# Attention weights turned for two heads at once: 64 places of the context per head, and the 13 left of eight heads together

## The chip, the core and the metric

The kernel runs on one core of a Trainium2 chip, in one launch, all in float32. The metric is the device time of the program in microseconds (us), as the median of several runs. Beside it there is one execution taken by the hardware profiler, with its own time and a trace of every instruction. The engines are called by the names of the profile: PE is TensorE's matmul and PEld its weight load, DVE is VectorE, ACT is ScalarE, POOL is GpSimd, SP the engine that only starts DMAs.

## The reference

Sixteen sequences of 128 rows of 128 numbers attend, with 16 heads of 8 numbers, to a context of 77 places of 96 numbers each. The result goes, behind a gate, into a mixture of four experts in four rounds, which the change does not touch. What it computes before that, cut to the attention:

```python
q = (einsum('bld,ed->ble', layernorm(x), Wq) + bq).reshape(b, l, 16, 8)
kv = (einsum('bmc,ec->bme', ctx, Wkv) + bkv).reshape(b, 77, 16, 16)
k, v = kv[..., :8], kv[..., 8:]
att = softmax(einsum('blhd,bmhd->blmh', q, k) / sqrt(8), axis=2)      # over the 77 places
out = einsum('blmh,bmhd->blhd', att, v).reshape(b, l, 128)
x = x + tanh(g_xattn) * (einsum('bld,ed->ble', out, Wo) + bo)
# then layernorm, and four rounds of: gate to 2 of 4 experts, gelu MLP 128 -> 512 -> 128, add
```

## The kernel before

The order of the work on PE, DVE and ACT is written out by hand: each engine runs its instructions in the order in which the program issues them, and so does GpSimd where the helper `gp` (line 88) records them. What one engine waits for from another is a semaphore.

The attention stage is a loop over the 16 sequences (line 1039), one round each, with the work of several sequences in flight. In round b:

- `spread_keys(b + 2)` on GpSimd makes `km`, the keys of a sequence once for each of four heads of a group, with the other heads' numbers zeroed (line 753).
- `turn_weights` (line 804) turns the weights of sequence b. `ex` holds, for 128 rows, 16 heads of 77 exponentials. PE transposes each head, 128x77 to 77x128, four heads to a bank of PSUM, and ACT copies each bank (77x512) to `exT`. The first two groups go before the scores of sequence b + 1, the other two after them. There are two banks for it (`bank_tr`), which `put_out` uses too.
- `scores(b + 1)` (line 766): four products of 32 rows, each in a group of rows of PE, two banks for each half.
- `put_out(b - 1)`: the output product of the sequence before; DVE adds it to x.
- `weights(b + 1)` (line 785), in two halves of eight heads: DVE takes the maximum of each head (L791), subtracts it into `ex` (L795), ACT takes the exponential in place (L801).
- `attend(b)` (line 811): 32 products of 77 places. Each puts 32 of the 128 rows of the result, so four of them stand side by side on PE. Half of them multiply by ones (`one`) and give the sums of the weights, half by the values (`vm`, in which the eight numbers of a head stand among zeros). Four heads of a group add up in one place of PSUM.
- `over_sums(b)` (line 829): DVE's reciprocal of the sums (L831) and the product with it (L833).

Work for later sequences is hung into the rounds with the lists `early` (between the first turned groups and the scores), `extra` (after the last turned group), `amid` and `behind` (after `attend` and after `over_sums`). There, each four sequences (i = 0 to 3) get their context turned (`turn_ctx`, line 710: four transposes, one copy by ACT into `ctxT`), their keys (`keys`, one product and one copy), queries and values (`values`, line 740: four products with the turned context as weights, four copies by ACT into `vm[i % 2]`). DVE and GpSimd also do, from round 7 on, the gate of the experts' first round. Products of these helpers take turns in two banks of PSUM (`bank`, line 114), so each new one waits until the one before the last has been read.

Before the loop the same helpers are called for the first four sequences (lines 846 to 876), with `warm` products that do nothing between them, and `spread_rows` (line 878) makes row constants: DVE copies them out (L885), ACT takes a tanh (`tg`, L886), DVE makes `bo_b` (L887), ACT copies `woT` and `wgT`.

Of the kernel before, what the change touches and what calls it, by code (L numbers as in the profile page):

```python
# [24 lines left out]
F32 = mybir.dt.float32  # L25
I32 = mybir.dt.int32
AF = mybir.ActivationFunctionType
ALU = mybir.AluOpType
# [3 lines left out]
P = 128  # L32
NH = 16
DH = 8
# [12 lines left out]
def gated_xattn_moe(  # L47
# [20 lines left out]
    nc = tc.nc  # L68
    B, L, D = x.shape
    M, C = ctx_768.shape[1:]  # L70
# [3 lines left out]
    BB = 4  # L74
    NB = B // BB
    TB = BB * L
# [18 lines left out]
    gp = Pinned()  # L95
# [29 lines left out]
    wkT = const.tile([C + 1, D], F32, name="wkT")  # L125
    wvT = const.tile([C + 1, D], F32, name="wvT")
# [8 lines left out]
    ident = const.tile([P, P], F32, name="ident")  # L135
# [34 lines left out]
    HG = 4  # L170
    NG = NH // HG
    GW = HG * DH
# [19 lines left out]
    akeep = ctx.enter_context(tc.tile_pool(name="akeep", bufs=1))  # L192


    vm = [akeep.tile([M, BB, HG * (D + DH)], F32, name=f"vm{i}") for i in range(2)]
    for i in range(2):
        nc.vector.memset(vm[i], 0.0)

    nc.vector.tensor_reduce(
        hmask,  # L200
        ident.rearrange("p (g k d) -> p k g d", k=HG, d=DH),
        AX.XY,
        ALU.add,
    )
    ctxT = akeep.tile([C + 1, B, M], F32, name="ctxT")
    gp.memset(ctxT[C : C + 1, :, :], 1.0)
    one = akeep.tile([M, HG, GW], F32, name="one")
    gp.memset(one, 0.0)
    for k in range(HG):
        gp.memset(one[:, k, ts(k, DH)], 1.0)  # L210
    gp.memset(blk, 0.0)


# [45 lines left out]
    awork = ctx.enter_context(tc.tile_pool(name="awork", bufs=2))  # L259

    def mm(*args, **kw):
        nc.tensor.matmul(*args, **kw)  # L262

    def tp(*args):
        nc.tensor.transpose(*args)  # L265
# [415 lines left out]
    ps = bank("ps_wkv")  # L681
# [28 lines left out]
    def turn_ctx(i):  # L710
        ps = bank("ps_ct")
        for j in range(BB):
            tp(ps[:C, ts(j, M)], ctx_sb[:, i * BB + j, :], ident[:M, :M])
        nc.scalar.copy(
            ctxT[0:C, ts(i, BB), :].rearrange("c b m -> c (b m)"), ps[:C, : BB * M]
        )

    def keys(i):
        ps = bank("ps_k")
        mm(  # L720
            ps[:, : BB * M], wkT, ctxT[:, ts(i, BB), :].rearrange("c b m -> c (b m)"),
            start=True, stop=True,
        )
        nc.scalar.copy(kT[:, ts(i, BB), :].rearrange("d b m -> d (b m)"), ps[:, : BB * M])

# [9 lines left out]
    def queries(i):  # L735
        ps = bank("ps_q")
        mm(ps, wqT, xnTs.pop(i), start=True, stop=True)
        nc.scalar.activation(qT[i], ps, AF.Identity, bias=bqc)

    def values(i):  # L740
        ps = bank("ps_v")
        for j in range(BB):
            mm(ps[:M, ts(j, D)], ctxT[:, i * BB + j, :], wvT, start=True, stop=True)
        for j in range(BB):

            nc.scalar.copy(
                vm[i % 2][:, j, :]
                .rearrange("m (k n) -> m k n", k=HG)[:, :, 0:D]
                .rearrange("m k (g n) -> m k g n", g=NG)[:, :, :, 0:DH],
                ps[:M, ts(j, D)].rearrange("m (g k d) -> m k g d", g=NG, k=HG),  # L750
            )
# [14 lines left out]
    def scores(b, km):  # L766


        q = qT[b // BB][:, ts(b % BB, L)]
        scs = []  # L770
        for u in range(2):
            sc = banks2("sc")
            for g in range(2):
                at = slice((2 * u + g) * GW, (2 * u + g + 1) * GW)
                mm(
                    sc[:, g, : HG * M],
                    q[at, :],
                    km[at, :, :].rearrange("d h m -> d (h m)"),
                    start=True,
                    stop=True,  # L780
                )
            scs.append(sc)
        return scs

    def weights(scs, then=None):

        ex = awork.tile([P, NH, M], F32, tag="ex", name="ex")
        for u, sc in enumerate(scs):
            sv = sc[:, :, : HG * M].rearrange("l g (h m) -> l g h m", m=M)
            mx = small.tile([P, 2, HG], F32, tag="mx", name="mx")  # L790
            beats.append(nc.vector.tensor_reduce(mx, sv, AX.X, ALU.max))  # L791
            if u and then:
                then()
            eu = ex[:, ts(u, 2 * HG), :]
            nc.vector.tensor_tensor(  # L795
                eu.rearrange("l (g h) m -> l g h m", h=HG),
                sv,
                mx.unsqueeze(3).to_broadcast([P, 2, HG, M]),
                ALU.subtract,
            )  # L800
            nc.scalar.activation(eu, eu, AF.Exp, scale=1.0 / math.sqrt(DH))  # L801
        return ex

    def turn_weights(ex, exT, groups):
        for g in groups:
            ps = bank_tr("ps_tr")
            for j in range(HG):
                tp(ps[:M, ts(j, L)], ex[:, g * HG + j, :], ident)
            nc.scalar.copy(exT[:, ts(g, HG), :].rearrange("m h l -> m (h l)"), ps[:M, :])  # L809

    def attend(b, exT):


        ps = bank("ps_av")
        for w in range(2):
            for k in range(HG):
                for g in range(NG):
                    at = slice(g * GW, (g + 1) * GW)
                    mm(
                        ps[at, ts(w, L)],  # L820
                        one[:, k, :] if w == 0
                        else vm[b // BB % 2][:, b % BB, k * D + g * GW : k * D + (g + 1) * GW],
                        exT[:, g * HG + k, :],
                        start=(k == 0),
                        stop=(k == HG - 1),
                    )
        return ps

    def over_sums(ps):
# [14 lines left out]


    turn_ctx(0)
    warm(2)
    keys(0)
    ps = bank("ps_cols")
# [21 lines left out]
    warm(4)  # L871
    scs = scores(0, kms.pop(0))
    values(0)
    turn_ctx(1)
    ex = {0: weights(scs)}
    keys(1)

# [41 lines left out]
    extra = {b: [] for b in range(B)}  # L919
# [119 lines left out]
    for b in range(B):  # L1039
        if b + 2 < B:  # L1040
            kms[b + 2] = spread_keys(b + 2)
        exT = awork.tile([M, NH, L], F32, tag="exT", name="exT")
# [12 lines left out]

        if b + 1 < B:
            ex[b + 1] = weights(scs, put_before)
        else:
            put_before()
        if b:  # L1060
            stats_x1(b - 1)
        ps_av = attend(b, exT)
        if b == B - 1:

            junk = const.tile([1, 1], F32, name="junk")
            nc.scalar.activation(junk, zero[0:1, 0:1], AF.Gelu_apprx_tanh)
            turn_half(0, 0, state[0]["c"])
        for f in amid[b]:
            f()
        o[b] = over_sums(ps_av)  # L1070
        for f in behind[b]:
            f()

        n = len(beats)
        for k in range(3):
            if (b, k) in stores_at:
                scatter(0, first["pos"], stores_at[b, k], stores, beats[n - 3 + k])
        if b == 14:
            load(0, stores)
# [280 lines left out]
```

## Time and profile before

| | |
|---|---|
| median of 3 runs | 449.91 us (449.91 to 450.17) |
| profiled execution, its own time | 448.24 us |
| its span, first to last instruction | 446.4 us |
| mean granted PE clock | 0.994 |
| attention stage, first turned weights to the last `over_sums` | about 19.3 to 115.8 us |

The page's first three parts:

```profile
PE 430.0 (96%) x4506; PEld 405.3 (91%) x4506; DVE 346.5 (78%) x918; ACT 274.8 (62%) x853; POOL 214.4 (48%) x249
PE   6899999998999999999999999999999999999991
DVE  8489998998866996897698689858867986774561
ACT  2567766766655666566666656666665666666661
POOL 5561926157005934752592377158426814650061
```

A digit is the busy share of a fortieth of the span, 11.16 us, in tenths. The attention stage is the first ten digits. A product in float32 is two records (two passes) in the trace, a transpose one. A record of PE lasts 0.27 us or more, but the next one starts much earlier, so the time of a row of products is read from their starts, as the chain of waits does.

The groups of instructions that the change touches, over the whole execution (columns: line, engine, operation, out<-in, shapes, count; busy us and mean ns of one; idle us before and what ended it):

```profile
L809 ACT COPY exT<-ps_tr 77x512 f32<-77x512 f32 x64 | 34.0, 581 | 13.4 <-PE ps_tr L265 13.1
L265 PE MATMUL ps_tr<-ident,ex 128*77 128x128 f32 x256 | 35.1, 280 | 1.1 <-ACT exT L809 1.1
L801 ACT ACTIVATE ex<-ex 128x616 f32<-128x616 f32 x32 | 23.0, 719 | 13.7 <-DVE ex L795 13.4
L791 DVE TENSOR_REDUCE mx<-sc 128x8 f32<-128x616 f32 x32 | 25.3, 790 | 5.8 <-PE sc L262 5.7
L795 DVE TENSOR_TENSOR ex<-sc,mx 128x616 f32<-128x616 f32 x32 | 25.4, 794 | 1.5
```

### The profile page before, as it was taken

To read this page: it belongs to the slowest core of one execution; us is meant where nothing else is said; L and a number is where in the kernel's file an instruction comes from. 1 tells how busy PE (TensorE), PEld (TensorE's weight loads), DVE (VectorE), ACT (ScalarE), POOL (GpSimd) and SP (SyncE) were. 2 spreads that over 40 slices of the span, in tenths; PEclk is the share of its full clock that TensorE was granted. 3 is DMA by queue.
4 is the path that set the end of the run, shared out by engine and by line. 5 is a ranking of instruction groups with operands and counts; after the bars stand their busy time and mean duration, and the time that the engine had idled before them with its cause. 6 is when DMAs were issued, how large, how long until landed. Compare 5 with 4: busy or idle time off the path is not lost.

```text
span 446.4 us, 12234 instructions
## 1 busy us (share of the span) xinstructions
PE 430.0 (96%) x4506; PEld 405.3 (91%) x4506; DVE 346.5 (78%) x918; ACT 274.8 (62%) x853; POOL 214.4 (48%) x249
## 2 busy tenths in 40 slices
PE   6899999998999999999999999999999999999991
PEld 6677888877899999999999999999999999999991
DVE  8489998998866996897698689858867986774561
ACT  2567766766655666566666656666665666666661
POOL 5561926157005934752592377158426814650061
PEclk9999999999999999999999999999999999999997
DMA  7520000012202301300130122014002201410000
GB/s 166 184 96 4 1 3 1 1 40 76 84 3 74 121 2 51 122 28 3 72 123 1 38 73 88 1 63 135 2 26 73 98 3 63 134 42 8 1 35 14
DMA packets 19553, 24.08 MB, mean 54 GB/s; under 512 B 3940, under 2 KB 16550, under 8 KB 19366
## 3 DMA queue, kind: packets, MB, share of 16 engines
q1 hardware_dynamic: 14868, 13.41, 9.6%
q0 software_dynamic: 3648, 9.71, 6.0%
q8 instruction: 36, 0.59, 0.5%
q10 hardware_dynamic: 978, 0.18, 0.2%
q14 instruction: 23, 0.19, 0.1%
HBM read 13.58 MB, written 9.71 MB: 52 GB/s over the span
## 4 chain that ended last, share of the span: by engine, by line
PE 71%; issue 9%; DVE 8%; POOL 6%; DMA 4%; ACT 1%; POOLq 0%; ACTq 0%; DVEq 0%
PE ps_y L262 28%; PE ps_h L262 28%; POOL out_dram L1124 4%; PE ps_av L262 4%; PE ps_tr L265 4%; DVE mx L791 2%; DMA wall<-in_L_ffn_W_dram 2%; DVE ex L795 2%; PE ps_c L265 2%; DVE rs L831 1%; PE sc L262 1%; DMA ctx_sb<-in_ctx_dram 1%; PE ps_bh L262 1%; DMA wq_n<-in_L_xattn_Wq_dram 1%; ACT exT L809 1%
## 5 line engine op out<-in xcount | busy, mean ns | idle before, releaser
L1096 ACT ACTIVATE hT<-ps_h,wb 128x128 f32<-128x128 f32 x512 | 145.9, 368 | 81.6 <-ACT hT L1096 56.7
L262 PE MATMUL ps_h<-curT,wb 128*128 128x128 f32 x1024 | 135.4, 275 | 0.7 <-ACT curT L379 0.7
L262 PE MATMUL ps_y<-wb,hT 128*128 128x128 f32 x1024 | 135.7, 276 | 0.0
L262 PEld LDWEIGHTS ps_h<-curT,wb 128*128 128x128 f32 x1024 | 124.6, 192 | 0.9 <-ACT curT L379 0.9
L262 PEld LDWEIGHTS ps_y<-wb,hT 128*128 128x128 f32 x1024 | 124.5, 192 | 0.0
L522 POOL DMA_INDIRECT sorted<-rows,pos_i x64 | 69.9, 1092 | 112.2 <-DVE start L515 49.3
L1015 DVE COPY wb<-wall 128x1028 f32 x128 | 105.4, 826 | 12.7 <-issue 6.5
L93 POOL TENSOR_TENSOR lp<-rows,wg_rows 128x512 f32<-128x512 f32 x48 | 75.3, 1593 | 29.7 <-DVE rows L1110 27.5
L1110 DVE SCALAR_TENSOR_TENSOR rows<-ps_y,pws,rows 128x128 f32<-128x128 f32 x126 | 43.6, 346 | 33.9 <-PE ps_y L262 33.9
L1096 ACT ACTIVATE hT<-ps_h,wall 128x128 f32<-128x128 f32 x160 | 45.7, 368 | 32.6 <-PE ps_h L262 32.6
L262 PE MATMUL ps_y<-wall,hT 128*128 128x128 f32 x320 | 43.1, 278 | 0.0
L262 PE MATMUL ps_h<-cx,wall 128*128 128x128 f32 x320 | 42.3, 275 | 0.0
L809 ACT COPY exT<-ps_tr 77x512 f32<-77x512 f32 x64 | 34.0, 581 | 13.4 <-PE ps_tr L265 13.1
L262 PEld LDWEIGHTS ps_y<-wall,hT 128*128 128x128 f32 x320 | 38.9, 192 | 2.7 <-ACT hT L1096 2.7
L262 PEld LDWEIGHTS ps_h<-cx,wall 128*128 128x128 f32 x320 | 38.9, 192 | 0.0
L265 PEld LDWEIGHTS ps_tr<-ident,ex 128*77 128x77 f32 x256 | 27.9, 147 | 10.1 <-ACT exT L809 7.8
L265 PE MATMUL ps_tr<-ident,ex 128*77 128x128 f32 x256 | 35.1, 280 | 1.1 <-ACT exT L809 1.1
L1124 POOL DMA_INDIRECT out_dram<-res,id_i x16 | 18.5, 1158 | 35.8 <-DVE res L1115 31.8
L419 DVE TENSOR_REDUCE lg<-lp 128x4 f32<-128x512 f32 x48 | 32.3, 674 | 3.4 <-POOL lp L93 3.4
L801 ACT ACTIVATE ex<-ex 128x616 f32<-128x616 f32 x32 | 23.0, 719 | 13.7 <-DVE ex L795 13.4
L791 DVE TENSOR_REDUCE mx<-sc 128x8 f32<-128x616 f32 x32 | 25.3, 790 | 5.8 <-PE sc L262 5.7
L795 DVE TENSOR_TENSOR ex<-sc,mx 128x616 f32<-128x616 f32 x32 | 25.4, 794 | 1.5
(170 smaller groups left out, 450.9 us busy)
## 6 DMA issues: line engine op xcount, KB each, us to landing
rows<-sorted SPq DMA_DIRECT2D x16, 528.0 KB
x_sb<-in_x_dram SPq DMA_DIRECT2D x4, 256.0 KB
wall<-in_L_ffn_W_dram SPq DMA_DIRECT2D x1, 1024.0 KB
wall<-in_L_ffn_W_dram SPq DMA_DIRECT2D x4, 256.0 KB
wg_rows<-wg_turned SPq DMA_DIRECT2D x1, 1024.0 KB
sorted<-rows,pos_i POOLq DMA_INDIRECT x64, 2.6
ctx_sb<-in_ctx_dram SPq DMA_DIRECT2D x4, 115.5 KB
out_dram<-res,id_i POOLq DMA_INDIRECT x16, 2.3
```

The costliest lines, as they stand in the source:

```text
L93: return lambda *a, **kw: tc.keep_in_program_order(f(*a, **kw))
L262: nc.tensor.matmul(*args, **kw)
L265: nc.tensor.transpose(*args)
L419: nc.vector.tensor_reduce(lgs[h][:, t, :], prods.pop((h, t)), AX.X, ALU.add)
L522: ins = nc.gpsimd.indirect_dma_start(out=sorted_rows[h], out_offset=bass.IndirectOffsetOnAxis(ap=pos_i[:, t : t + 1], axis=0), in_=rows[h] ...
L791: beats.append(nc.vector.tensor_reduce(mx, sv, AX.X, ALU.max))
L795: nc.vector.tensor_tensor(eu.rearrange("l (g h) m -> l g h m", h=HG), sv, mx.unsqueeze(3).to_broadcast([P, 2, HG, M]), ALU.subtract,)
L809: nc.scalar.copy(exT[:, ts(g, HG), :].rearrange("m h l -> m (h l)"), ps[:M, :])
L1015: nc.vector.tensor_copy(wb, wall[:, ds(e, 1), :].rearrange("p o n -> p (o n)"))
L1096: nc.scalar.activation(hT[:, fc, :], ps[:, ts(fc, P)], AF.Gelu_apprx_tanh, bias=wb[:, W_B + fc : W_B + fc + 1],)
L1110: return nc.vector.scalar_tensor_tensor(at, y, w, at, ALU.mult, ALU.add)
L1124: ins = nc.gpsimd.indirect_dma_start(out=out_rows, out_offset=bass.IndirectOffsetOnAxis(ap=id_i[:, t : t + 1], axis=0), in_=res, in_offset ...
```

## The change

The 77 places of a head are split into 64 and 13. The exponentials are written in that order: first 64 places of each of 16 heads, then the 13 left of each. So two heads stand side by side in 128 columns, and eight heads' remainders in 104.

- `weights`: DVE subtracts into a tile `d` of its own. ACT takes three exponentials in place of two: 512 columns for each half, and 208 for what is left, after the second half.
- `turn_weights`: 4 transposes of 128 columns (heads 0 to 7), after the scores 4 more (heads 8 to 15), then 2 of 104 columns. ACT copies 128x512, 128x512 and 104x256.
- `attend`: 12 products for the sums and 12 for the values, each over 128 or 104 rows. The values of two heads stand in the two halves of the rows of `vm`, and `vr` holds the values for the places left of eight heads, zeros outside of each head's own columns; `one` and `one_r` are the same with ones.
- `turn_ctx`: the turned context is written twice for the first 64 places, and eight times for the 13 left, by two copies of ACT; `ctxT` is now two tiles that take turns.
- `values`: four products of 128 columns, and eight copies of 64 rows in place of four of 77. `values_left` is new: four products of 104 columns, and a multiplication with `one_r`. For the first four sequences DVE does it from PSUM, before the first maximum; for the others ACT copies to a tile `left` and GpSimd multiplies. It is hung into rounds 2, 5 and 9.
- At the start DVE clears two tiles `vm` of 1152 in place of 2176 columns, and GpSimd makes `one_r` with a memset and two selects.

```diff
-    vm = [akeep.tile([M, BB, HG * (D + DH)], F32, name=f"vm{i}") for i in range(2)]
+    MP = P // 2
+    MR = M - MP
+    HR = NH // 2
+    HP = HG // 2
+    vm = [akeep.tile([P, BB, HP * (D + 2 * DH)], F32, name=f"vm{i}") for i in range(2)]
+    vr = [akeep.tile([HR * MR, BB, D], F32, name=f"vr{i}") for i in range(2)]
...
+    CT = 2 * MP + HR * MR
+    ctxT = [akeep.tile([C + 1, BB, CT], F32, name=f"ctxT{i}") for i in range(2)]
...
-        nc.scalar.copy(
-            ctxT[0:C, ts(i, BB), :].rearrange("c b m -> c (b m)"), ps[:C, : BB * M]
-        )
+        pv = ps[:C, : BB * M].rearrange("c (b m) -> c b m", m=M)
+        cv = ctxT[i % 2][0:C, :, :]
+        for lo, n, m0, m1 in ((0, 2, 0, MP), (2 * MP, HR, MP, M)):
+            nc.scalar.copy(
+                cv[:, :, lo : lo + n * (m1 - m0)].rearrange("c b (n m) -> c b n m", n=n),
+                pv[:, :, m0:m1].unsqueeze(2).to_broadcast([C, BB, n, m1 - m0]),
+            )
...
+    def values_left(i, eng=None):
+
+        ps = bank("ps_vr")
+        for j in range(BB):
+            mm(
+                ps[: HR * MR, ts(j, D)], ctxT[i % 2][:, j, 2 * MP : CT], wvT,
+                start=True, stop=True,
+            )
+        v = ps[: HR * MR, :].rearrange("m (b d) -> m b d", d=D)
+        if eng is None:
+            eng = gp
+            left = awork.tile([HR * MR, BB, D], F32, tag="left", name="left", bufs=1)
+            nc.scalar.copy(left, v)
+            v = left
+        eng.tensor_tensor(
+            vr[i % 2], v, one_r.unsqueeze(1).to_broadcast([HR * MR, BB, D]), ALU.mult
+        )
...
-        ex = awork.tile([P, NH, M], F32, tag="ex", name="ex")
+        ex = awork.tile([P, NH * M], F32, tag="ex", name="ex")
+        left = ex[:, NH * MP :].rearrange("l (h m) -> l h m", m=MR)
+        d = awork.tile([P, NH, M], F32, tag="d", name="d", bufs=1)
...
-            nc.scalar.activation(eu, eu, AF.Exp, scale=1.0 / math.sqrt(DH))
+            nc.scalar.activation(
+                ex[:, ts(u, HR * MP)].rearrange("l (h m) -> l h m", m=MP),
+                d[:, ts(u, HR), 0:MP], AF.Exp, scale=1.0 / math.sqrt(DH),
+            )
+        nc.scalar.activation(left, d[:, :, MP:M], AF.Exp, scale=1.0 / math.sqrt(DH))
         return ex
 
-    def turn_weights(ex, exT, groups):
-        for g in groups:
-            ps = bank_tr("ps_tr")
-            for j in range(HG):
-                tp(ps[:M, ts(j, L)], ex[:, g * HG + j, :], ident)
-            nc.scalar.copy(exT[:, ts(g, HG), :].rearrange("m h l -> m (h l)"), ps[:M, :])
+    def turn_weights(ex, exT, u):
+
+        ps = bank_tr("ps_tr")
+        if u < 2:
+            for j in range(HR // 2):
+                tp(ps[:, ts(j, L)], ex[:, ts(u * HR // 2 + j, 2 * MP)], ident)
+            nc.scalar.copy(exT[:, ts(u, TB)], ps)
+        else:
+            for j in range(2):
+                at = NH * MP + j * HR * MR
+                tp(ps[: HR * MR, ts(j, L)], ex[:, at : at + HR * MR], ident)
+            nc.scalar.copy(exT[: HR * MR, 2 * TB :], ps[: HR * MR, : 2 * L])
...
     values(0)
+    values_left(0, nc.vector)
     turn_ctx(1)
...
-    extra[2] += [lambda: queries(1)]
+    extra[2] += [lambda: queries(1), lambda: values_left(1)]
...
-        extra[b + 1] += [lambda i=i: keys(i)]
+        extra[b + 1] += [lambda i=i: keys(i), lambda i=i: values_left(i)]
...
-        turn_weights(ex[b], exT, (0, 1))
+        turn_weights(ex[b], exT, 0)
...
-        turn_weights(ex.pop(b), exT, (2, 3))
+        turn_weights(ex[b], exT, 1)
+        turn_weights(ex.pop(b), exT, 2)
```

More of the change, by code (lines that the diff above doesn't have):

```diff
@@ L204, in gated_xattn_moe @@
     )
-    ctxT = akeep.tile([C + 1, B, M], F32, name="ctxT")
-    gp.memset(ctxT[C : C + 1, :, :], 1.0)
-    one = akeep.tile([M, HG, GW], F32, name="one")
+    CT = 2 * MP + HR * MR
+    ctxT = [akeep.tile([C + 1, BB, CT], F32, name=f"ctxT{i}") for i in range(2)]
+    gp.memset(ctxT[0][C : C + 1, :, :], 1.0)
+    one = akeep.tile([P, HP, GW], F32, name="one")
     gp.memset(one, 0.0)
-    for k in range(HG):
-        gp.memset(one[:, k, ts(k, DH)], 1.0)
+    for j in range(HP):
+        for k in range(2):
+            gp.memset(one[ts(k, MP), j, ts(2 * j + k, DH)], 1.0)
+    one_r = akeep.tile([HR * MR, D], F32, name="one_r")
+    gp.memset(one_r, 1.0)
+    for base, sign in ((0, 1), (MR - 1, -1)):
+        gp.affine_select(
+            out=one_r, in_=one_r, compare_op=ALU.is_ge, fill=0.0, base=base,
+            pattern=[[0, 2], [-sign * MR, HR], [0, DH]], channel_multiplier=sign,
+        )
+    gp.memset(ctxT[1][C : C + 1, :, :], 1.0)
     gp.memset(blk, 0.0)
@@ L720, in keys @@
         mm(
-            ps[:, : BB * M], wkT, ctxT[:, ts(i, BB), :].rearrange("c b m -> c (b m)"),
-            start=True, stop=True,
+            ps[:, : BB * M].rearrange("d (b m) -> d b m", m=M), wkT,
+            ctxT[i % 2][:, :, MP : MP + M], start=True, stop=True,
         )
@@ L742, in values @@
         for j in range(BB):
-            mm(ps[:M, ts(j, D)], ctxT[:, i * BB + j, :], wvT, start=True, stop=True)
+            mm(ps[:, ts(j, D)], ctxT[i % 2][:, j, 0 : 2 * MP], wvT, start=True, stop=True)
         for j in range(BB):
[L746 to L750, printed above, removed]
-            )
+            for k in range(2):
+                nc.scalar.copy(
+                    vm[i % 2][ts(k, MP), j, :]
+                    .rearrange("m (j n) -> m j n", j=HP)[:, :, k * DH : k * DH + D]
+                    .rearrange("m j (g n) -> m j g n", g=NG)[:, :, :, 0:DH],
+                    ps[ts(k, MP), ts(j, D)]
+                    .rearrange("m (g j k d) -> m k j g d", g=NG, j=HP, k=2)[:, k],
+                )
[5 more added lines that the diff above has]
+                start=True, stop=True,
+            )
+        v = ps[: HR * MR, :].rearrange("m (b d) -> m b d", d=D)
[7 more added lines that the diff above has]
+        )
     def spread_keys(b):
@@ L793, in weights @@
                 then()
-            eu = ex[:, ts(u, 2 * HG), :]
             nc.vector.tensor_tensor(
-                eu.rearrange("l (g h) m -> l g h m", h=HG),
+                d[:, ts(u, HR), :].rearrange("l (g h) m -> l g h m", h=HG),
                 sv,
@@ L800, in weights @@
             )
-            nc.scalar.activation(eu, eu, AF.Exp, scale=1.0 / math.sqrt(DH))
-        return ex
-    def turn_weights(ex, exT, groups):
-        for g in groups:
-            ps = bank_tr("ps_tr")
-            for j in range(HG):
-                tp(ps[:M, ts(j, L)], ex[:, g * HG + j, :], ident)
-            nc.scalar.copy(exT[:, ts(g, HG), :].rearrange("m h l -> m (h l)"), ps[:M, :])
+            nc.scalar.activation(
+                ex[:, ts(u, HR * MP)].rearrange("l (h m) -> l h m", m=MP),
+                d[:, ts(u, HR), 0:MP], AF.Exp, scale=1.0 / math.sqrt(DH),
+            )
@@ L811, in attend @@
     def attend(b, exT):
         ps = bank("ps_av")
+        i, j = b // BB % 2, b % BB
         for w in range(2):
-            for k in range(HG):
+            for k in range(HP + 1):
                 for g in range(NG):
                     at = slice(g * GW, (g + 1) * GW)
[L819 to L826, printed above, removed]
+                    if k < HP:
+                        v = vm[i][:, j, k * D + g * GW : k * D + (g + 1) * GW]
+                        weights, lo = one[:, k, :] if w == 0 else v, (g * HP + k) * L
+                        moving = exT[:, lo : lo + L]
+                    else:
+                        weights = one_r[:, at] if w == 0 else vr[i][:, j, at]
+                        lo = 2 * TB + g // 2 * L
+                        moving = exT[: HR * MR, lo : lo + L]
+                    mm(ps[at, ts(w, L)], weights, moving, start=(k == 0), stop=(k == HP))
@@ L1041, in gated_xattn_moe @@
             kms[b + 2] = spread_keys(b + 2)
-        exT = awork.tile([M, NH, L], F32, tag="exT", name="exT")
-        turn_weights(ex[b], exT, (0, 1))
+        exT = awork.tile([P, 2 * TB + 2 * L], F32, tag="exT", name="exT")
+        turn_weights(ex[b], exT, 0)
         for f in early[b]:
```

## The prediction

> **What bounds the kernel now.** I read the page's second part first: the attention stage is the first ten or so of its 40 slices, and the rest belongs to the experts, which the change does not touch. Then I took the chain of waits in order of time, to see which engine carries the attention rounds.
>
> ```profile
> 40.69 1.88 PE ps_av L262 x64
> 42.58 1.03 PE ps_tr L265 x8
> 43.60 0.73 PE sc L262 x8
> 44.34 1.03 PE ps_tr L265 x8
> ...
> 95.33 0.70 DVE mx L791
> 96.03 0.26 DVE rows L840
> 96.29 0.71 DVE ex L795
> ```
>
> The reader is to see two parts: TensorE carries the chain from 23 to 66 us, without a break; VectorE carries nearly all of it from 66 to 108.6, with GpSimd in between at 67.9 to 73.9. So before asking what TensorE saves I asked how much room VectorE has. The busy times of the engines in stretches, cut at each round's reciprocal (columns: stretch, its length, then PE, weight loads, DVE, ACT, POOL):
>
> ```profile
> 36.87:42.64 5.77, 5.77 (x99) 4.87 (x100) 5.28 (x11) 4.23 (x11) 0.00 (x0) 1.00 0.00 0
> 59.71:65.92 6.21, 6.21 (x104) 5.30 (x104) 5.71 (x13) 4.71 (x12) 0.00 (x0) 1.00 0.00 0
> 79.15:85.91 6.76, 6.76 (x103) 5.38 (x102) 6.45 (x15) 4.55 (x9) 2.10 (x2) 1.00 0.01 2
> ```
>
> VectorE is busy 5.28 of 5.77 us, and in the order of its instructions the round 36.87 to 42.64 has one wait, 0.26 at its end. Its own length is therefore 5.77 - 0.26 = 5.51 us. What the whole change can give lies in VectorE's waits for TensorE, read from VectorE's timeline:
>
> ```profile
> 15.54 0.80 DVE L791 TENSOR_REDUCE mx<-sc 128x8 f32<-128x616 f32 x1 [3.44 <-PE sc L262]
> ...
> 21.20 0.80 DVE L791 TENSOR_REDUCE mx<-sc 128x8 f32<-128x616 f32 x1 [0.80 <-PE sc L262]
> ...
> 25.21 0.96 DVE L831 RECIPROCAL rs<-ps_av 128x128 f32<-128x128 f32 x1 [0.85 <-PE ps_av L262]
> ...
> 27.41 0.80 DVE L791 TENSOR_REDUCE mx<-sc 128x8 f32<-128x616 f32 x1 [0.49 <-PE sc L262]
> ```
>
> After these come, from the same timeline, 0.24 (36.87), 0.26 (42.64), 0.36 (55.69), 0.24 (59.71), 0.25 (65.92) and 0.64 (68.54); from 74 on none for TensorE until the experts start.
>
> **TensorE, each round.** Before: 16 transposes of 77 columns and 32 products of 32 columns, two passes each. After: 8 transposes of 128 columns, 2 of 104, and 24 products. The first transposes of a group start 0.109 us apart (1.03 for 8 with a start of about 0.17); the 128-column transposes of normalised rows (ps_c, 0.44 for 4 in the chain) have the same step. So 6 fewer save 0.65. The products run four side by side, one such set in about 0.11 (1.88 for 64 passes, 16 sets); four sets fewer save 0.44. Together 1.09 us a round.
>
> [...]
>
> **Does VectorE then run without a wait?** Take its reciprocal as zero in a round. The last subtraction for this round ended at -0.41 (L795, 0.80). The second exponential is now 512 wide: from 0.719 for 616 to about 0.63, ends at +0.25. The new one for the 13 places left, 208 wide, costs about 0.38 (fixed part by the 77x128 copies, 0.27), ends +0.55. ACT's three copies of turned weights follow it in its queue: 0.59 each for 128x512 (as xnT, 0.589), about 0.37 for 104x256, done at +1.95. TensorE's sums and values start at about 1.9, take 1.31 plus a start, end by 3.4. The next reciprocal is due at 5.51: two us of cover. Products put between (values left, 8 passes at 0.11 = 0.88, with queries 0.86, or with keys 0.52 and a group of rows 0.44) take up to 1.84 of that; cover 0.2 to 0.3. ACT a round: 4 x 0.58 + 2 x 0.72 = 3.76 before, 3.2 after, so its extra copies (left 0.59; the second context copy about 0.6; eight value copies for four, +0.3) fit. If that cover were gone, each such round would cost its shortfall, 0.2 to 0.5, four times.
>
> GpSimd gets three multiplications, near x_sb<-x_sb,bo_b 128x512 (1.30 each). Queued behind the first are the 4.08 us of keys and then km, which is due for the scores at 43.5: by the sum left is copied at 35.7, multiply to 37.0, constants 0.8, keys 4.1, km to 42.6. It fits by 0.9. Behind the second (52.0 to 53.3) stand rows for the first routing, due 60.7, then ready by 58.4. Cost nothing, taken; up to 0.5 if left is late.
>
> **Waits that go.** 0.24 + 0.26 + 0.36 + 0.24 + 0.25 = 1.35 us. The 0.64 at 68.54 is not counted: from the scale at 67.65 VectorE next needs GpSimd's result at 73.86 for its normalisation, and GpSimd is busy all that time:
>
> ```profile
> 67.90 1.04 POOL L93 TENSOR_TENSOR rstda<-rstda,half 128x4 f32<-128x4 f32 x1 [9.80 <-DVE lg L397]
> 69.04 1.57 POOL L93 TENSOR_SCALAR rows<-x_sb,mva,rstda 128x128 f32<-128x128 f32 x2
> 70.58 0.70 POOL L93 TENSOR_TENSOR km<-kT,hmask 128x308 f32<-128x308 f32 x1
> 71.27 1.56 POOL L93 TENSOR_SCALAR rows<-x_sb,mva,rstda 128x128 f32<-128x128 f32 x2
> 72.81 1.02 POOL L93 TENSOR_TENSOR rstdf<-rstdf,half 128x4 f32<-128x4 f32 x1
> ```
>
> The wait moves there. From 74 to the output product of round 15 (TensorE 115.87, released by VectorE's 0.29 after its last reciprocal) VectorE has no wait to lose; turned weights and products that end earlier in round 15 only wait for it. So the tail gives nothing.
>
> **What the start costs.** The multiplication of the first batch's left values stands on VectorE ahead of the first maximum. TensorE does scores to 15.5, values 0.88, then the new values left 0.88, landing at 17.45. The multiply is 104x512 from PSUM; between 128x128 (0.29) and 616 (0.79) it is about 0.69, with ends 0.55 and 0.79. The first maximum moves from 15.54 to 18.1, +2.56. The two maxima and subtractions take 3.17 and end at 21.27. ACT: second exponential 0.63, left 0.38, kT 0.40, tg 0.20, to 22.7 with their overlaps of 0.1; bo_b 0.35 on VectorE, to 23.0. The maximum of 21.20 so starts at 23.0, +1.8: its wait of 0.80 and most of the 1.2 us before are eaten. The exT copies, behind woT (which waits for bo_b), come at 23.4 to 24.8, and TensorE ends the first sums at 26.1; VectorE arrives at 26.2, so of 0.84 nothing is left and the shift is +1.0. At 27.41 the 0.49 goes too: **+0.5**. On ACT the eight value copies (1.0 to 1.4) and two context copies (1.15) delay keys and row constants to about 21.2, just beside VectorE, no further cost. The earlier part is even: memsets of 1152 instead of 2176 elements free VectorE 0.6 us sooner, ACT spends that on the second context copy.
>
> **Sum.** +0.5 - 1.35 = -0.85, taken as **-0.8 us**. Against the profiled execution: span 446.4 to 445.6, its time 448.24 to 447.4. The median of the runs shown is 449.91, 1.67 above that execution; the same difference gives **449.1**.
>
> **Rivals.**
> 1. *The start is hidden* (0.15): if VectorE's multiply and the copies cost nothing by 27.4, the waits of 0.84 and 0.49 go as well: -1.35 - 1.33 = -2.7, 447.2. For it speaks that VectorE idled about 2 us between 18.7 and 21.2; against it that ACT's tg and exT are chained behind the exponentials.
> 2. *The start is not absorbed; slower* (0.17): the multiply ahead of the first maximum delays it by 2.56 and the chain exponential, tg, bo_b, exT passes all of it on. Then +2.56 - 1.35 = +1.2, 451.1. It decides from a shift of 1.35 at the maximum of 27.41 (before); I have 0.5.
> 3. *TensorE does not get shorter* (0.13): 128-column transposes cost by columns, and rounds with values left lose what the others gain: -0.85 + 0.7 = about 449.8 to 450.0.
> 4. The change does what it says; that it builds more work than named I could exclude from the order of instructions.
>
> TensorE will idle about a fifth of each round. [...]
>
> **Numbers.** The likeliest, VectorE takes over and the start costs half a microsecond, has 0.55: 449.1, own range 448.4 to 449.8. 0.2% is 0.9 us, about what a measurement of this kernel can tell from no change: below 449.0 lies some half of the likeliest and rival 1, 0.43; within, 0.39; above 450.8 rival 2, 0.18. The range, 447.6 to 451.0, takes in most of both rivals.
>
> **What would show it.** VectorE's waits for ps_av and sc gone from 30 to 66; the first maximum at 18.1; the reciprocal of the first round near 26.2; a VectorE wait of 0.7 to 0.8 for rstdf before its normalisation; 0.109 between 128-column transposes. It is wrong if the reciprocals still wait for TensorE, if the first maximum of round 1 is later than 24, or if GpSimd's km comes after the scores want it.

## The result, and the profile after

The changed kernel takes **452.10 us** (median of 6 runs, 451.16 to 452.47), the kernel before in the same session 449.86 (6 runs, 448.20 to 450.17): a ratio of 1.0051, interval 1.0034 to 1.0069. It is slower by half a per cent, and above the top of the range forecast, 451.0. The profiled execution of the changed kernel took 452.22, with a span of 450.5 where the one before had 446.4; its mean granted PE clock (the share of full speed at which TensorE was let run) is 0.981 where the other had 0.994. In medians the change costs 2.2 us, in the profiled pair 4.1; the gap between the two is taken up below.

The clock row of the page after, tenths of full speed in fortieths of the span:

```profile
PEclk9869999999999999999999999999999999999996
```

Two low digits, in the first 34 us. The view by windows of the same execution (length, then busy us and count of PE, weight loads, DVE, ACT, POOL; then the granted clock, DMA share, GB/s), cut where the granted clock changes, and once more at 20.40, 3.41 us ahead of the second drop:

```profile
6.75:10.16 3.41, 1.32 (x8) 0.72 (x6) 2.84 (x15) 2.48 (x5) 1.29 (x2) 1.00 0.76 184
10.16:13.58 3.42, 3.42 (x17) 3.42 (x17) 1.65 (x7) 0.57 (x3) 2.84 (x4) 0.50 0.99 325
...
20.40:23.82 3.42, 1.51 (x9) 0.92 (x9) 3.35 (x5) 2.24 (x6) 0.00 (x0) 1.00 0.00 0
23.82:30.64 6.82, 6.82 (x59) 4.88 (x62) 3.77 (x7) 3.83 (x11) 4.33 (x19) 0.50 0.25 101
```

From 10.16 to 13.58 and from 23.82 to 30.64 us TensorE runs at half clock, each time behind a stretch in which it has little to do (1.32 busy of 3.41, and 1.51 of 3.42). PE's timeline shows what it waits for there (start, us, instruction, idle before it and what ended that):

```profile
9.24 0.76 PE L283 MATMUL ps_k<-ctxT,wkT 97*128 97x308 f32 x2 [2.09 <-issue]
...
21.11 0.47 PE L286 MATMUL ps_ct<-ident,ctx_sb 77*96 77x77 f32 x4 [0.95 <-ACT vm L772]
22.79 0.79 PE L283 MATMUL ps_k<-ctxT,wkT 97*128 97x308 f32 x2 [1.21 <-ACT ctxT L738]
```

The first keys wait for the turned context, which ACT now copies twice (1.12 us for both, 0.41 before), and stand at 9.24 where they stood at 8.26. The second idle stretch was one of 0.89 us before, ahead of the next keys; now the next context needs a bank of PSUM that ACT's eight value copies free (1.74 us in all, 0.22 apart), and its keys wait for two copies. VectorE's timeline, the rows to set beside those of 15.54, 21.20, 25.21, 27.41, and then of 73.86, before:

```profile
20.19 0.69 DVE L794 TENSOR_TENSOR vr<-ps_vr,one_r 104x512 f32<-104x512 f32 x1 [8.28 <-PE ps_vr L283]
20.80 0.79 DVE L839 TENSOR_REDUCE mx<-sc 128x8 f32<-128x616 f32 x1
...
27.31 0.80 DVE L839 TENSOR_REDUCE mx<-sc 128x8 f32<-128x616 f32 x1 [1.40 <-PE sc L283]
...
31.33 0.96 DVE L890 RECIPROCAL rs<-ps_av 128x128 f32<-128x128 f32 x1 [0.85 <-PE ps_av L283]
...
33.07 0.80 DVE L839 TENSOR_REDUCE mx<-sc 128x8 f32<-128x616 f32 x1
...
77.22 1.49 DVE L276 TENSOR_SCALAR rows<-rows,mvf,rstdf 128x128 f32<-128x128 f32 x4 [0.89 <-POOL rstdf L93]
...
84.89 1.42 DVE L470 TENSOR_TENSOR hot<-rank 128x128 f32<-128x128 f32 x1
```

The maximum of 27.41 comes at 33.07, 5.66 later: that is the loss. From there to 77.22 VectorE has no wait for TensorE, and the lag falls to 3.36: 2.30 won in the rounds. `hot`, 0.77 us at 81.52 before, takes 1.42. From 85 us on the lag is 4.0 to 4.1, to the end.

### The profile page after: what moved, and what is told of

The parts are those of the page before. It is cut to its first block, busy times and chain, and to the rows that moved or that the text cites. A ratio compares the mean times of both kernels' runs of the same rounds, so it can differ in the third digit from the quotient of the medians.

```text
span 450.5 us, 11638 instructions
## 1 busy us (share of the span) xinstructions
PE 425.7 (94%) x4186; PEld 396.5 (88%) x4186; DVE 345.2 (77%) x919; ACT 273.9 (61%) x876; POOL 220.2 (49%) x256
## 3 DMA queue, kind: packets, MB, share of 16 engines
HBM read 13.58 MB, written 9.71 MB: 52 GB/s over the span
## 4 chain that ended last, share of the span: by engine, by line
PE 66%; DVE 15%; issue 9%; POOL 6%; DMA 2%; ACT 1%; POOLq 0%; DVEq 0%; SPq 0%
PE ps_y L283 28%; PE ps_h L283 28%; POOL out_dram L1185 4%; DVE mx L839 4%; DVE d L842 4%; PE ps_warm L283 2%; DVE rs L890 2%; PE ps_c L286 2%; PE ps_bh L283 1%; DVE st L268 1%; DMA rows<-sorted 1%; DVE oT L892 1%; DVE rows L899 1%; POOL rows L93 1%; DMA sorted<-rows,pos_i 1%
## 5 line engine op out<-in xcount | busy, mean ns | idle before, releaser
L848 ACT ACTIVATE ex<-d 128x512 f32<-128x512 f32 x32 | 20.3, 637 | 20.6 <-DVE d L842 20.4
L286 PEld LDWEIGHTS ps_tr<-ident,ex 128*128 128x128 f32 (+1 forms) x160 | 17.6, 144 | 16.6 <-ACT ex L848 9.0
L286 PE MATMUL ps_tr<-ident,ex 128*128 128x128 f32 (+1 forms) x160 | 26.6, 294 | 5.4 <-ACT ex L848 4.8
L842 DVE TENSOR_TENSOR d<-sc,mx 128x616 f32<-128x616 f32 x32 | 25.4, 794 | 1.6
L1171 DVE SCALAR_TENSOR_TENSOR rows<-ps_y,pwxs,rows 128x128 f32 x40 | 14.0, 350 | 14.8 <-PE ps_y L283 13.9
```

The costliest lines, as they stand in the source:

```text
L842: nc.vector.tensor_tensor(d[:, ts(u, HR), :].rearrange("l (g h) m -> l g h m", h=HG), sv, mx.unsqueeze(3).to_broadcast([P, 2, HG, M]), ALU ...
L848: nc.scalar.activation(ex[:, ts(u, HR * MP)].rearrange("l (h m) -> l h m", m=MP), d[:, ts(u, HR), 0:MP], AF.Exp, scale=1.0 / math.sqrt(DH),)
L1171: return nc.vector.scalar_tensor_tensor(at, y, w, at, ALU.mult, ALU.add)
```

## The experiments

Theory A was that the clock alone made the change slower, the rival that the change itself costs and its start is what hurts. The first four were run together on one chip, four more later on the same chip, the last four on another one. The kernel before took 452.54, 452.59 and 452.18 there (medians), with 450.66 to 450.76 as its lowest.

**e1_fill.** The changed kernel with `warm` products, which compute nothing that is used, in the idle stretches of its start (`warm_tr` is the same product in a bank of `bank_tr`):

```diff
     turn_ctx(0)
-    warm(2)
+    warm(10)
...
     values_left(0, nc.vector)
+    warm_tr(4)
     turn_ctx(1)
+    warm_tr(5)
```

> The changed kernel with products that do nothing in the idle stretches of TensorE at the start: 8 more before the first keys, 4 before and 5 after the second context is turned; nothing else moves. Theory A (the clock): TensorE ran at half clock from 10.3 to 13.5 and from 23.8 to 30.7 us because it had idled 2.1 us at 7.2 and 2.6 us at 20.1; with the gaps filled the clock stays at 1.00, the first maximum comes at 19.0 in place of 20.8, and the time is 452.1 - 3.5 = 448.6 (448.0 to 449.6). Theory B (the queues): the multiply, the value copies and the second context copy alone made the loss; the time stays at 451.5 to 452.5.

Measured: 448.39 us (447.77 to 449.01), ratio to the kernel before 0.9918 (0.9896 to 0.9941), clock 0.993. Its start is at full clock throughout, and the longest idle stretch listed for TensorE from 5 to 29 us is 0.40.

**e2_early.** The first values and values left go into VectorE's idle stretch ahead of the turned rows, copied by VectorE, in the place of 8 of 10 warm products:

```diff
     load_experts()
-    warm(10)
+    values(0, nc.vector, bank_tr)
+    values_left(0, nc.vector, bank_tr)
+    warm(2)
...
-    values(0)
-    values_left(0, nc.vector)
```

> The changed kernel with the first four sequences' values and left values moved up into the stretch before the first rows are turned: TensorE does them in place of 8 of the 10 products that do nothing, VectorE (idle from 12 to 20 us) does their copies and the multiply. Theory B: the first maximum follows the scores directly, 2.6 us sooner, the second context is copied 2 to 3 us sooner, time 449.0 to 449.8. Theory A: the row of products stays at half clock, so the scores come as late as 17.3; what the shorter idle stretch at 20 saves decides the rest, time 450 to 451.

Measured: 450.13 us (445.10 to 454.05, 20 runs), ratio 0.9941 (0.9919 to 0.9963), mean clock 0.979, half clock at 10 to 16 and 23 to 27 us.

**e3_keys.** The context is copied once for the keys; `spread_ctx`, behind them, makes the copies for the values from SBUF:

```diff
-        for lo, n, m0, m1 in ((0, 2, 0, MP), (2 * MP, HR, MP, M)):
...
+        nc.scalar.copy(cv[:, :, MP : MP + M], ps[:C, : BB * M].rearrange("c (b m) -> c b m", m=M))
...
+    def spread_ctx(i):
+        cv = ctxT[i % 2][0:C, :, :]
+        nc.scalar.copy(cv[:, :, 0:MP], cv[:, :, MP : 2 * MP])
+        nc.scalar.copy(
+            cv[:, :, MP + M : CT].rearrange("c b (n m) -> c b n m", m=MR),
+            cv[:, :, 2 * MP : MP + M].unsqueeze(2).to_broadcast([C, BB, HR - 1, MR]),
+        )
```

> The changed kernel with the context copied once for the keys first (308 columns, one copy, as before the change) and spread for the values afterwards from SBUF. The first keys start at about 8.5 in place of 9.24. If the 2.1 us of idle TensorE before them is what drops the clock (theory A), the half clock at 10.3 goes too and the time is 449.5 to 450.0; if only the queue counts (theory B) it is 0.7 less, 451.4, and more ACT work at the start may take some of that.

Measured: 450.97 us (448.02 to 454.30, 22 runs), ratio 0.9952 (0.9926 to 0.9978), clock 0.976. The first keys did come 0.7 us earlier (8.54), and the time lies between the two that were expected; half clock at 10 to 13 and 23 to 27 us. So the half clock stayed when the gap ahead of the keys shrank from 2.09 to 1.61:

```profile
8.54 0.76 PE L283 MATMUL ps_k<-ctxT,wkT 97*128 97x308 f32 x2 [1.61 <-issue]
```

**e4_both.** e2 and e3 together, the second context spread in round 1.

> Both edits of the two kernels before it, and the second context spread in round 1 in place of ahead of the first exponentials. Scores at 14.7 to 15.5 as before the change and the first maximum directly after; from there VectorE runs without waits. Both theories: 446.5 to 448 if the clock stays at 1.00, about 448.5 to 449.5 if one half-clock window remains; below 449.9 it beats both kernels.

Measured: 450.78 us (449.00 to 454.10, 14 runs), ratio 0.9972 (0.9942 to 1.0003), clock 0.978, half clock at 9 to 15 and 22 to 29 us. The second stretch at half clock comes here behind a gap of only 0.51 us. The three shorter starts have half clock in their profiles and times spread over 5 to 9 us; e1, which shortens nothing, has neither. One execution of e2 had a mean clock of 0.994: it took 445.10.

**e5_before_fill, e6_after_again, e7_fill_again.** The kernel before with the same warm products (8, 4 and 5 more, at the same places), the changed kernel as it is, and e1 again.

> The kernel before with the same warm products in the idle stretches of its start (8 more ahead of the first keys, 4 between the values and the second context's turn, 5 behind it). Its start had no stretch of half clock in the profile, so there is nothing to win but what its own executions lose now and then. Theory A (clock alone made the change slower; at full clock the change is worth about 2.5 us): times tight, within 0.5 us of the fastest executions of the kernel before in the same session, and 2 to 3 us ABOVE the changed kernel with the same products. Rival B (the warm products help any version, the change itself costs): 2 us or more below the kernel before, and level with or below the changed kernel with the same products. Granted clock 0.994 to 0.996 by both.

> The changed kernel as it is, beside the others on one chip. Theory A: granted clock 0.980 to 0.984 with half clock near 10 to 13 and 24 to 31 us, 3 to 4 us above the same kernel with warm products. Rival B: within 1.5 us of it.

> The changed kernel with the warm products of e1, repeated so that it stands beside the two kernels before and after on one chip. Theory A: 448.4 +- 0.7, clock 0.992 to 0.995, a ratio to the kernel before with warm products of 0.994 to 0.996. Rival B: a ratio of 1.000 to 1.004 to it.

Measured: 451.64 (451.57 to 454.78; ratio 0.9984, 0.9961 to 1.0008), 452.52 (450.39 to 454.44; 1.0001, 0.9982 to 1.0021) and 448.33 (447.67 to 450.67; 0.9918, 0.9893 to 0.9944). The warm products take 4.2 us off the changed kernel; the other gains nothing that its interval can tell, and is 3.3 slower than the changed one with them. VectorE's timeline of e7 is the changed kernel at full clock:

```profile
18.57 0.69 DVE L800 TENSOR_TENSOR vr<-ps_vr,one_r 104x512 f32<-104x512 f32 x1 [6.66 <-PE ps_vr L283]
...
24.15 0.80 DVE L845 TENSOR_REDUCE mx<-sc 128x8 f32<-128x616 f32 x1
...
27.24 0.94 DVE L896 RECIPROCAL rs<-ps_av 128x128 f32<-128x128 f32 x1
...
28.88 0.80 DVE L845 TENSOR_REDUCE mx<-sc 128x8 f32<-128x616 f32 x1
```

28.88 where the first profile of the changed kernel had 33.07, 4.19 earlier, and e6's has 32.64. The medians of e6 and e7 are 4.19 apart, their profiled spans 4.2; of that, 3.76 is there at this maximum, and 0.4 more comes at 114 to 121 us, where e6 has one more stretch at half clock. In e6's start half clock lies at 8.3 to 15.2 and 25.4 to 28.8 us, and not, as expected, where it lay in the first profile. Theory A holds, but two numbers of it missed. e5 was to lie within 0.5 of the kernel before at its best (450.75) and lies 0.9 above, because there the nine products behind the values push the row constants back (`rows_b` waits 1.78 for TensorE, 0.88 without them). So e5 is also 3.3 above e7, where 2 to 3 was expected; without its own 0.9 it would be 2.4.

**e8_order.** e1's warm products, and the new products put where warm products stood; VectorE copies the values as in e2:

```diff
     load_experts()
-    warm(10)
+    warm(3)
     turn_x(0)
-    warm(3)
+    values(0, nc.vector, bank_tr)
     queries(0)
-    warm(4)
+    values_left(0, nc.vector, bank_tr)
     scs = scores(0, kms.pop(0))
-    values(0)
-    values_left(0, nc.vector)
     turn_ctx(1)
+    warm_tr(5)
```

> The changed kernel with warm products and its start in another order: the four value products run between the turned rows and the queries, the values left between the queries and the scores (they stand where warm products stood), VectorE copies them in its idle stretch, and only 3 warm products stay ahead of the turned rows. If the start's path is turned rows, queries, scores, first maximum, with nothing else behind it, the turned rows go from 12.4 to about 10.8 us, the scores from 15.7 to about 14.5, the first maximum from 19.16 to about 15.4 (the multiplication lies ahead of it, hidden), and the fourth maximum (28.86 in e1) comes 1.5 to 3 us earlier: 445.4 to 447.0. If instead a later row sets the end (GpSimd's chain at 66 to 73 us runs by its own clock), less than 1 us is gained: 447.4 to 448.4. If the clock falls in the shorter stretches that are left, 449 or more.

Measured: **444.09 us** (443.70 to 445.94), ratio 0.9823 (0.9798 to 0.9849), clock 0.993, more than was expected. VectorE's timeline:

```profile
14.30 0.69 DVE L801 TENSOR_TENSOR vr<-ps_vr,one_r 104x512 f32<-104x512 f32 x1
14.97 0.80 DVE L846 TENSOR_REDUCE mx<-sc 128x8 f32<-128x616 f32 x1
...
24.68 0.80 DVE L846 TENSOR_REDUCE mx<-sc 128x8 f32<-128x616 f32 x1
```

The multiplication is still ahead of the first maximum and now in the shadow of the scores. The fourth maximum is 4.2 us ahead of e7's, and the time 4.2 below: here the start passes on to the end in full.

**e9_before_order.** The kernel before with that start, `values(0)` between the turned rows and the queries, the other warm products as in e8.

> The kernel before with the start of e8: warm products ahead of the first keys, the value products between the turned rows and the queries, nothing between the scores and the second context's turn but its own wait, filled. It asks whether e8's gain belongs to the start alone, which the kernel before could have had too. If the weights turned for two heads are worth what the rounds show (VectorE's waits for TensorE gone: about 2.3 us between the fourth maximum and the normalisation of rows 4 to 7), this kernel gains 0.5 to 1.5 us over the kernel before (fourth maximum at 26.0 to 27.0 where it was 27.41) and stays 4 to 6 us above e8: 448.5 to 450.5. If the start alone makes e8 fast, it comes within 1.5 us of e8: 445.5 or less.

Measured: 449.70 us (449.25 to 450.27), ratio 0.9951 (0.9932 to 0.9971). Against the median of the kernel before (452.18) that is 2.5 us, against its lowest time (450.66) 1.0, and 1.0 as well between the profiled spans (e12's 448.9 to 447.9). So with both at full clock the new order alone is worth about 1 us to the kernel before; e8, on the other chip, is 5.6 us faster than it.

**e10_apart and e11_both.** Two waits of e8 that have to do with GpSimd. e10 puts the residual of the last four sequences one round earlier in its queue, e11 also (the last two lines) the rows of the last two of four sequences behind its root for `rstdf`:

```diff
-        extra[i * BB - 1] += [lambda i=i: residual(i)]
+        extra[i * BB - (2 if i == 3 else 1)] += [lambda i=i: residual(i)]
...
-        early[b] += [lambda i=i: norm_x(i, gp, (2, 3))]
+        (behind if i == 3 else early)[b] += [lambda i=i: norm_x(i, gp, (2, 3))]
```

> e8 with GpSimd's addition of the residual for rows 12 to 15 put one round earlier in its queue, so that it no longer runs beside VectorE's product for the places (hot<-rank, 1.42 us beside it, 0.77 alone). If that neighbourhood is the cause: hot at 0.77, VectorE 0.65 earlier from there to the end, 443.4 +- 0.3. If the changed layout makes it slow (its operands' places), hot stays at 1.4 and the time at 444.1.

> e10, and GpSimd's rows for the blocks 14 and 15 put behind its root for the rows 4 to 7, for which VectorE waits 0.89 us (rstdf). If GpSimd's chain sets that wait: the wait falls to under 0.2, the normalisation comes 0.7 to 0.9 us earlier, 442.6 +- 0.4. If a wait for TensorE or ACT lies just behind it, under 0.3 us is gained over e10.

Measured: 442.75 (442.19 to 443.51; ratio 0.9792, 0.9769 to 0.9816) and **441.83** (441.62 to 446.57; 0.9801, 0.9764 to 0.9838). The line of `hot` in e10's VectorE timeline, and the normalisation in e11's:

```profile
76.44 0.39 DVE L470 TENSOR_TENSOR hot<-rank 128x128 f32<-128x128 f32 x1
```

```profile
67.26 1.39 DVE L276 TENSOR_SCALAR rows<-rows,mvf,rstdf 128x128 f32<-128x128 f32 x4
```

Alone, `hot` takes 0.39 us, not the 0.77 that I had taken for its price: the kernel before already ran it partly beside that addition. In e11 the wait of 0.89 is gone (no bracket is left), and the median falls by 0.92, though the times of the two overlap. e11 beats both kernels, by 8.8 us against the lowest time of the kernel before on that chip.

**e12_before_look.** The kernel before as it is, profiled on the chip of e9 to e11.

> The kernel before, profiled on this chip, where its undisturbed executions take 450.8 to 452.6 and not the 448.24 of its first profile. If the difference is TensorE's (a pause, or half clock, which the kernel before cannot hide since VectorE waits for TensorE in its rounds), VectorE shows waits for TensorE of 1 to 3 us in sum that the first profile has not, at one or two places; then the changed kernel, whose VectorE does not wait for TensorE, is spared them. If it lies in the experts' stage or the tail, the first product of the experts stands at 114.9 as in the first profile and the end is later.

It took 450.71, span 448.9, clock 0.995, and so is one of the fastest executions there, not the usual one. VectorE's timeline there, and then the same two rows in the first profile before:

```profile
99.26 0.96 DVE L831 RECIPROCAL rs<-ps_av 128x128 f32<-128x128 f32 x1 [1.41 <-PE sc L262]
...
101.15 0.79 DVE L573 TENSOR_TENSOR y<-start,edge 128x42 f32<-128x42 f32 x1
```

```profile
97.54 0.94 DVE L831 RECIPROCAL rs<-ps_av 128x128 f32<-128x128 f32 x1
...
99.42 0.19 DVE L573 TENSOR_TENSOR y<-start,edge 128x42 f32<-128x42 f32 x1
```

Up to there the two are within 0.2 us. Then VectorE waits 1.41 for TensorE, whose eight records of scores take 1.51 us in place of 0.80 (1.36 in e5, at a granted clock of 1.00), between two scatters of GpSimd; and the small product beside the next scatter takes 0.79 in place of 0.19. Together with the 0.2 this is 2.3 of the 2.5 between the two spans. e5 and e9 show the same wait (1.49, 1.43). In the first profile of the changed kernel two groups of scores of that stage (100.72 and 106.84 us) take 1.20 in place of 0.80 too, and one in e7 (102.63), but VectorE waits for none of them, and its small product takes 0.19 and 0.20.

## Why the prediction was wrong

Against its own base, the profiled execution, I forecast -0.8 and the profiled pair shows +4.1. The parts, in the prediction's order:

**The clock: the step that failed.** The sum adds nothing for the clock. I took the 1.00 of the rows of before over to the changed kernel, also that of the row of the attention stage in which TensorE is idle longest:

```profile
108.93:114.50 5.57, 4.39 (x81) 3.32 (x79) 4.69 (x12) 4.17 (x8) 1.51 (x2) 1.00 0.60 197
```

I held no gap of after to be long enough to change it. Two things are wrong with that step. The rows of before could not bear it out, since they belong to another program. And how long a gap must be was a guess of mine that no run had shown. The gaps of after were 2.09 us, and 0.95 and 1.21 close together, and half clock followed in both profiles of that start (after and e6).

The granted clock holds each value for whole multiples of one length. From 6.75 us on, after has 1.00 for 3.41 us, 0.50 for 3.42, 1.00 for 10.24 (three times 3.41) and 0.50 for 6.82 (two times). In e6's start half clock lasts two such stretches and then one, and full clock follows for 25 (28.80 to 114.14). What within a stretch makes the clock fall, the runs do not show. The length of a gap alone does not: the kernel before idles 2.31 us ahead of its first keys, and its clock stayed at 1.00:

```profile
8.26 0.76 PE L262 MATMUL ps_k<-ctxT,wkT 97*128 97x308 f32 x2 [2.31 <-DVE st L247]
```

```profile
4.25:7.66 3.41, 1.70 (x16) 1.45 (x15) 3.27 (x12) 1.35 (x2) 0.41 (x5) 1.00 0.95 221
```

If stretches of 3.41 us are counted from 4.25, where the full clock of that profile begins, the end of one divides the gap: 1.71 us lie in the row shown and 0.60 behind it; in after all 2.09 lie in one. That this kept the clock of before is an estimate, and e3 does not bear it out, for there 1.61 us in one stretch were followed by half clock. Nor does the busy time sort the stretches: e3's of 6.28 to 9.69 has 1.80 busy, and half clock behind it, the row above 1.70, and full clock. What the runs do show is that there is no half clock where the gaps are filled: in e1's start none over 0.40 us is left, and every row has 1.00. Half clock cost **4.2 us** (e6 to e7 in the medians, 4.19 from the first profile after to e7 at the fourth maximum). That is most of the 5.66 of the start, and more than all of the loss.

**The start at full clock: right in form, 1.0 us too short.** The multiplication took 0.69 as taken from its neighbours, and moved the first maximum by its 2.6. But the sentence "The earlier part is even" was wrong: the second context copy stands ahead of the first keys, and PE's queue carries their delay (9.24 to 8.26, 1.0 us) into everything behind it. 0.7 of it is the copy (e3, without it: 8.54). Of the rest 0.2 is not the change's: in e12 the kernel before runs as much later than in its first profile (its first maximum at 15.75, not 15.54). All four times in e7 are so much later than forecast: 19.18 (18.1), 24.15 (23.0), 27.24 (26.2), and 28.88 where 27.9 was worked out. So +1.5 in place of +0.5. The eight value copies took 1.74 where 1.0 to 1.4 was taken; at full clock that set nothing, since `bo_b` waited for `tg`, which stood behind ACT's exponentials and key copy (0.56 us, to 23.72 in e7), and the constants were there before (23.16). One of the prediction's own signs of being wrong, a first maximum of round 1 later than 24, came true (27.31, and 24.15 at full clock). Rival 2, whose mechanism is a start that is not absorbed, said that it decides from a shift of 1.35 at the maximum of 27.41: at full clock the shift was 1.47 against the first profile, but 1.26 against e12's (27.62), so that the runs do not decide it. The time is near its 451.1, but not by its sum: without the clock's share e7's span, 446.6, is level with the first profile's 446.4, since the rounds gave more.

**The rounds: the mechanism held, the gain was mis-sized.** VectorE waits for TensorE nowhere from 33 to 72 us, the step between 128-column transposes is 0.109 (47.448, 47.557, 47.666), the same as for 77 columns before (42.677, 42.786, 42.896), so rival 3 falls, and with it the thought that the transposes cost by their columns. No run shows the 0.7 us that it adds: in the rounds with added products VectorE does not wait for TensorE. ACT's new rows cost 0.637, 0.367, 0.580 and 0.377 where 0.63, 0.38, 0.59 and 0.37 were taken. But the sum from the fourth maximum to the normalisation is -2.30 where -1.35 was forecast. VectorE's own round is 5.26 us (36.79 to 42.05), not 5.51: of the 0.51 between it and 5.77 the view had listed 0.26 as a wait; 0.08 more of delay at the same reciprocal, 0.11 ahead of the maximum and 0.04 in the reciprocal itself went too. Subtracting only the listed waits gave too long a round.

**GpSimd's chain: right.** The wait went to `rstdf`, 0.89 where 0.7 to 0.8 was forecast, and e11 shows that the order of its queue sets it.

**A collision that was not in the sum: +0.65.** With VectorE in another phase, `hot` ran wholly beside GpSimd's addition, where before it had the start to itself and the addition paid (1.43 in place of 1.27).

So in the profiled pair +5.66 (4.19 clock, 1.47 start), -2.30 and +0.65 make +4.0 of the 4.1.

**The base.** I carried the 1.67 us between the profiled execution and the median before over to the changed kernel. But the profiled execution, 448.24, is as fast as the fastest of six runs (448.20), and the other five take 449.76 to 450.17; the changed kernel's, 452.22, lies at its own median. So the two medians differ by 2.2 and not by 4.1. What the other five paid was not profiled on that chip. TensorE's pause in round 13 and the slow small product of e12, 2.0 us together, would fit in size, and the changed kernel, with slack on TensorE, is spared them (after and e7); that the five paid just this is not shown. On the two chips of the experiments most executions of the kernel before pay something else besides: they take 452.1 us or more at a mean clock of 0.992 or less, where the others take 450.7 to 451.6 at 0.993 to 0.995. From 0.995 to the usual 0.991 is about 1.8 of 450 us of clock; one stretch of 3.41 us at half clock, of the kind that e6 shows at 114.14, loses 1.7. So by estimate they have one such stretch more; none of them was profiled. Between executions at full clock the change is worth about 2.4 us (450.75, the lowest of the kernel before, to 448.33, e7's median), where 0.8 was forecast.

**Open.** What makes TensorE pause in round 13, and by what the granted clock falls: neither the length of a gap nor the busy time of a stretch of 3.41 us sorts what these traces show.

## What to carry to other kernels

A change that gives the tensor engine less to do, or puts copies ahead of its products, has to be checked for the clock of the changed program, and the rows of the one before do not answer for it: here the granted clock fell to 0.50 behind two stretches of 3.41 us in the start that were busy for 1.32 and 1.51, and that cost 4.2 us. Fill such idle stretches with products, best with ones that have to be done anyway (e8: 8.4 us in the median against the changed kernel alone, where warm products alone gave 4.2). Warm products in the changed kernel are also the quickest test of whether a loss is the clock's. And where the profiled execution is not near the median, find out what the usual execution pays, and at which mean clock, before a difference is worked out on top of it.

## What the runs showed of the hardware

- The granted clock of after was 1.00 or 0.50, each held for whole multiples of 3.41 us (one, one, three and two of them from 6.75 to 30.64). It fell to 0.50 behind gaps of 2.09 us (after) and 1.61 us (e3) and stayed at 1.00 behind one of 2.31 us (before) and where no gap was over 0.40 us (e1's start). At 0.50 the step between 128-column transposes was 0.213 us (24.872, 25.085 and 25.299 in after), where it was 0.109 at 1.00.
- A product on VectorE with both operands in SBUF (`hot`, 128x128) took 0.39 us alone (e10) and 1.42 us beside GpSimd's 128x512 addition (after); in the kernel before, VectorE being first, 0.77 and the addition 1.43 in place of 1.27.
- TensorE took 1.51 us for one group of eight records of scores that otherwise take 0.80 (round 13 in e12); in e5 1.36 and for two groups of after 1.20, these at a granted clock of 1.00. The cause is not seen.
